# A fused attention and adapter kernel: the exchange of maxima and totals between two key classes moves to VectorE, and work is placed otherwise in two of its gaps

## The chip, the cores and the metric

The kernel runs on one core of a Trainium2 chip. The metric is the device time of one execution in microseconds (us). Five engines work side by side, each through its own queue in order: TensorE (PE; its weight loads are shown as PEld), VectorE (DVE), ScalarE (ACT), GpSimd (POOL) and the DMA queue (SP). They wait for each other by semaphores.

## The reference

Four sequences of 1024 tokens with 1024 features go through two blocks with a residual each, all in fp32:

```python
x = x + attn(layernorm(x), wq, wk, wv, wo)      # 32 heads of 32, rotary, causal softmax
x = x + ffn(layernorm(x), route_w, A, Bw)

# attn
q, k, v = split(x @ wq), split(x @ wk), split(x @ wv)
q, k = rotary(q), rotary(k)
scores = where(causal, q k^T / sqrt(32), min)
out = (softmax(scores) @ v) @ wo
# ffn: the best of 8 experts, weighted with its logit, rank 16
logits = x @ route_w^T
h = x @ A^T                                     # 8 experts x 16
out = (onehot(argmax(logits)) * max(logits) * h) @ Bw
```

## The kernel before

**Units.** The attention is cut into 32 units: 4 sequences of 8 groups of 4 heads. A unit has 16 query tiles `t` of 64 queries. Tile `t` has (t+1)*64 keys, and these are split in two classes, the even and the odd blocks of 32 keys. The 128 partitions of a score tile are two halves of 32 queries by two key classes: partition group `i = 2*half + odd` holds 32 queries against one class, and group `i ^ 1` holds the same queries against the other class. So the maximum and the total of a row of softmax each have to be joined from two partition groups. Tiles 0 to 7 make block 0 and tiles 8 to 15 block 1.

**A unit's slots.** `SLOTS` lists eleven slots of a unit. Nine are score rounds, `score_round` for one to four tiles: TensorE makes the scores (L381) in PSUM tile `s`, of which there is one; ScalarE copies them to SBUF (L392); GpSimd adds the causal mask on the diagonal (L395). Slot "second" multiplies block 1 of the unit before with its values (L565, in the same PSUM tile) and slot "first" block 0 of the unit itself. Numbered from 0, "second" is slot 2 and "first" slot 8; slot 3 has tiles 9, 2, 1 and 0.

**Softmax.** After a round, `find_tops` has VectorE reduce the negated maxima (L413) for the tiles that are complete. Four GpSimd copies of 32 partitions (L428) put each group's maxima into the partitions of the other class (`other`). In the next slot `join_tops` takes the minimum of both on VectorE (L433) and releases the tile's exponentials into `to_exp`. `exponentiate_some` issues them on ScalarE (L440) by a share, with their sums accumulated into `den`. `turn_probabilities` transposes them on VectorE (L465) at the beginning of a slot.

**Totals.** When all tiles of a block have been transposed, `join_sums` starts a generator, `sums_steps`. Its first half copies `den` across the classes on GpSimd (L505, four copies). Its second half runs in the next slot, from `go_on_with_sums`: VectorE adds (L507) and takes the reciprocal (L508) of 32 values a partition, and four GpSimd copies (L512) spread them to `by`. `spread_sums` turns `by` on TensorE (L539) behind the value product, ScalarE copies it back (L540), and `scale_values` multiplies on VectorE (L585) into `at`. As the value product lies in tile `s`, the next score round on TensorE waits for L585.

**What fills the gaps.** The list `todo` holds steps for TensorE: for the first sequence only the projections of the next unit, six chains of 8 steps (q, k for the first half of the tokens, q, k for the second, v for both; L295). A q or k chain ends with an eviction on ScalarE, two VectorE operations (L325, L327) and two GpSimd products of 128x512 (L326, L328) for the rotary embedding. `fill` runs a share of what is left of `todo` in each slot; for units 0 to 6 the share of slot r is `LENGTHS[r] / sum(LENGTHS[r:])`, for all others the slots count alike. In the later sequences `todo` also holds the output projection and the adapter of the sequence before. With two pieces of the value product ("second"), three steps are run between them.

**Norm of the next sequence.** The first four token tiles of sequence 1 are loaded at the start of unit 6. `Norm.scale(t)` finds the moments up to tile t+1 (VectorE, with one GpSimd power for each tile) and scales up to tile t. In unit 6, all four are scaled at once, as the `meanwhile` of `apply` in slot "first" (L981): behind the value product and ahead of `scale_values`. `turn` transposes them at the beginning of unit 7.

Of the kernel before, what the change touches and what calls it, by code (L numbers as in the profile page):

```python
# [9 lines left out]
F32 = mybir.dt.float32  # L10
AF = mybir.ActivationFunctionType
ALU = mybir.AluOpType
AX = mybir.AxisListType

P = 128
# [4 lines left out]
SQ = 32  # L20
# [6 lines left out]
    ((7, 0, 512), (6, 0, 448)),  # L27
    ((5, 0, 384), (4, 0, 320), (3, 0, 256)),
    "second",
    ((9, 0, 640), (2, 0, 192), (1, 0, 128), (0, 0, 64)),  # L30
    ((15, 0, 1024),),
    ((14, 0, 960),),
    ((13, 0, 896),),
# [11 lines left out]

LENGTHS = (1.6, 1.6, 0.5, 0.8, 0.8, 0.8, 0.8, 1.7, 1.4, 1.1, 1.3)


class Step:
# [20 lines left out]
def tile_preln_attn_then_top1_lora(  # L72
# [17 lines left out]
    nc = tc.nc  # L90
# [4 lines left out]
    HD = D // HEADS  # L95
# [303 lines left out]

    places, tops, dens = {}, {}, {}  # L400
    ended = []
    to_exp, to_turn, to_join, to_join_exp = deque(), [], [], []

    def find_tops(u):

        if not ended:
            return
        n = len(ended)
        top = small.tile([P, n, HG], F32, tag=f"top{n}", name=f"top_{u}_{ended[0]}", bufs=3)
        for k, t in enumerate(ended):  # L410
            step = HG if t < QT else 2
            for h in range(0, HG, step):
                nc.vector.tensor_reduce(  # L413
                    top[:, k, h : h + step],
                    places[u, t][:, h : h + step, :],
                    AX.X,
                    ALU.max,
                    negate=True,
                )
            tops[u, t] = top[:, k, :]  # L420
            if (u, t // QT) not in dens:
                dens[u, t // QT] = small.tile(
                    [P, QT, HG], F32, tag="den", name=f"den_{u}_{t // QT}", bufs=3
                )
        other = small.tile([P, n, HG], F32, tag=f"other{n}", name=f"other_{u}_{ended[0]}", bufs=2)
        for i in range(P // SQ):
            k = i ^ 1
            nc.gpsimd.tensor_copy(other[k * SQ : (k + 1) * SQ], top[i * SQ : (i + 1) * SQ])  # L428
        to_join.append((top, other))

    def join_tops():
        for top, other in to_join:
            nc.vector.tensor_tensor(top, top, other, ALU.min)  # L433
        to_join.clear()
        to_exp.extend(to_join_exp)
        to_join_exp.clear()

    def exponentiate(u, t, h):
        pr = places[u, t]
# [53 lines left out]
        ]  # L493
        return store, loads

    pending, wides = deque(), {}

    def sums_steps(u, blk):


        den = dens.pop((u, blk))
        other = small.tile([P, QT, HG], F32, tag="oden", name=f"oden_{u}_{blk}", bufs=2)
        for i in range(P // SQ):
            k = i ^ 1
            nc.gpsimd.tensor_copy(other[k * SQ : (k + 1) * SQ], den[i * SQ : (i + 1) * SQ])  # L505
        yield
        nc.vector.tensor_tensor(den, den, other, ALU.add)  # L507
        nc.vector.reciprocal(den, den)  # L508
        wides[u, blk] = by = big.tile([P, TB, P], F32, tag="by", name=f"by_{u}_{blk}")
        for i in range(P // SQ):  # L510
            rows = slice(i * SQ, (i + 1) * SQ)
            nc.gpsimd.tensor_copy(  # L512
                by[rows].rearrange("p t (h d) -> p t h d", d=HD),
                den[rows].rearrange("p (t c) h -> p c t h", c=2)[:, i % 2]
                .unsqueeze(3)
                .to_broadcast([SQ, TB, HG, HD]),
            )
        yield

    begun = set()  # L520

    def join_sums(u, blk):

        if (u, blk) in begun or any((u, t) in places for t in range(blk * QT, (blk + 1) * QT)):
            return
        begun.add((u, blk))
        pending.append(sums_steps(u, blk))
        next(pending[-1])

    def go_on_with_sums():  # L530
        while pending:
            next(pending.popleft())

    def spread_sums(u, blk):

        by = wides.pop((u, blk))
        pt = bank([P, TB, P], f"pr_{u}_{blk}")
        for i in range(TB):
            nc.tensor.transpose(pt[:, i, :], by[:, i, :], eye_sb)  # L539
        nc.scalar.copy(by, pt)  # L540
        return by.rearrange("p t k -> p (t k)")
# [259 lines left out]
    for u, (b, g) in enumerate(units):  # L801
        project, new_tail = [], []
        if b:
            fetch, (project,), new_tail = finish_steps(
                b - 1, g, "resident" if u == len(units) - 1 else "stream"
            )
            if g:
                between[-1].insert(max(0, len(between[-1]) - 8), fetch)
            else:
                late_fetch[u] = fetch  # L810

        if u + 1 < len(units) and g + 1 == NG:
            if b:
                homes = {0: "q", 1: "k", 3: "q", 4: "k"}
                norm = Norm(b + 1, {0: (3,), 1: (4,), 2: (6,), 5: (7,)}, homes)
                steps = change_steps(u + 1, norm, project, tail)
            else:
                norm = Norm(b + 1, {0: (5,), 1: (6,), 2: (7,)}, {4: "k"})  # L820
                between[-1].insert(0, Step(lambda norm=norm: norm.load(*range(TB)), 0.0))
                steps = [norm.turning(t) for t in range(TB)] + begin_steps(u + 1, norm, [])
            norms[b + 1] = norm
        else:
            steps = []
            if u + 1 < len(units):
                for n, tb in (("q", 0), ("k", 0), ("q", 1), ("k", 1), ("v", 0), ("v", 1)):
                    steps += chain(u + 1, n, tb)
            if not steps:
                steps = list(project)  # L830
            elif b and not g:
                steps = steps[:36] + weave(steps[36:], project)
            else:
                steps = weave(steps[:-6], project) + steps[-6:]
            if u + 1 == len(units):
                new_tail6 = tail
            n = len(steps)
            for k, s in reversed(list(enumerate(tail))):
                steps.insert(6 + k * n // 7, s)
        between.append(steps)  # L840
        tail = new_tail
# [85 lines left out]
    def apply(u, blk, meanwhile=lambda: None):  # L927
        while any((u, t) in places for t in range(blk * QT, (blk + 1) * QT)):
            exponentiate_some(1)
            turn_probabilities()  # L930
        join_sums(u, blk)
        go_on_with_sums()
        avs, pieces = value_pieces(u, blk)
        for k, piece in enumerate(pieces):
            piece()
            turn_probabilities()
            if k == 0:
                meanwhile()
            if k < len(pieces) - 1:
                exponentiate_some(VALUE_SHARE)  # L940
                do_some(APART_BY)
        by = spread_sums(u, blk)
        exponentiate_some(VALUE_SHARE)
        stores.append(scale_values(u, blk, avs, by))
# [9 lines left out]
    for u, (b, g) in enumerate(units):  # L954
# [6 lines left out]
            ends_at = second  # L961
        for r, pieces in enumerate(SLOTS):
            if pieces in ("first", "second"):
                join_tops()
            if pieces == "second":
                if u == final:
                    todo.extend(early)
# [9 lines left out]
                    meanwhile()  # L977
                stores.append(put)
            elif pieces == "first":
                if b == 0 and g + 2 == NG:  # L980
                    apply(u, 0, lambda: norms[1].scale(TB - 1))  # L981
                else:
                    apply(u, 0)
            else:
                join_tops()
                turn_probabilities()
                go_on_with_sums()
                if second < r < first_:
                    join_sums(u, 0)
                score_round(u, pieces)  # L990
                if r == second - 1 and u:
                    while any((u - 1, t) in places for t in range(QT, 2 * QT)):
                        exponentiate_some(1)
                        turn_probabilities()
                    join_sums(u - 1, 1)
                find_tops(u)
                exponentiate_some(SHARE / 3)
                to_join_exp.extend((u, t, h) for t in ended for h in range(HG))
                ended.clear()
                if r in (second + 1, first_ + 1):  # L1000
                    for put in stores:
                        put()
                    stores.clear()
                    if u == final and r == first_ + 1:
                        load_adapter()
                if r == second + 2:
                    scatter(loads, 2)
                    if u in late_fetch:
                        do(late_fetch[u])
                        for k in range(3 if b == 1 else 0):  # L1010
                            load_chunk(k)
# [11 lines left out]
                held_back,  # L1023
                0.0 if pieces in ("first", "second") else SHARE * 2 / 3,
            )
    join_tops()
    while to_exp:
        exponentiate_some(SHARE)
        turn_probabilities()
# [57 lines left out]
```

## Time and profile before

| | us |
|---|---|
| time, median of 3 runs (range) | 2867.87 (2865.06 to 2869.86) |
| the profiled execution: its time, its span | 2865.45, 2863.7 |
| busy: TensorE | 2718.6 (95%) |
| busy: VectorE | 1959.8 (68%) |
| busy: ScalarE | 1745.7 (61%) |
| busy: GpSimd | 1082.9 (38%) |
| VectorE waits for GpSimd's masks (L413 for L395) | 434.0, 193 times |
| VectorE waits for GpSimd's copies of maxima (L433 for L428) | 125.2, 138 times |
| first score matmul, last start of one | 65.4, 2757.9 |

The span is cut into units by the first score matmul of each. Units 0 to 6 begin at 65.4, 135.5, 210.5, 287.6, 362.8, 437.5 and 513.6 us, unit 7 at 599.6, unit 8 at 682.5. Units 8 to 14, 16 to 22 and 24 to 30 last 82 to 83 us each; the units with a change of sequence (15 and 23) 113.4 and 115.8 us.

How to read it: a busy share over the whole span hides that the sequences have different limits. The table of windows shows them apart. Where TensorE is busy nearly all of a window at full clock, only less work for it can shorten the window; where it is not, the list of its waits says who was late. The last column but two of a window line is the granted clock of TensorE, 1.00 at full speed.

### The profile page before, as it was taken

To read this page: it belongs to the slowest core of one execution; us is meant where nothing else is said; L and a number is where in the kernel's file an instruction comes from. 1 tells how busy PE (TensorE), PEld (TensorE's weight loads), DVE (VectorE), ACT (ScalarE), POOL (GpSimd) and SP (SyncE) were. 2 spreads that over 40 slices of the span, in tenths; PEclk is the share of its full clock that TensorE was granted. 3 is DMA by queue.
4 is the path that set the end of the run, shared out by engine and by line. 5 is a ranking of instruction groups with operands and counts; after the bars stand their busy time and mean duration, and the time that the engine had idled before them with its cause. 6 is when DMAs were issued, how large, how long until landed. Compare 5 with 4: busy or idle time off the path is not lost. (4 is left out here: it accounts for less than half of the span.)

```text
span 2863.7 us, 85129 instructions
## 1 busy us (share of the span) xinstructions
PE 2718.6 (95%) x35328; PEld 1343.4 (47%) x35328; DVE 1959.8 (68%) x3169; ACT 1745.7 (61%) x5006; POOL 1082.9 (38%) x2500
## 2 busy tenths in 40 slices
PE   8888898979999999998999999998999999999998
PEld 5344444444444444544445444444444445444445
DVE  3676666687776677777676776677667677776545
ACT  2676767756666666655666666664566666666421
POOL 3444444334334434333434334443344334334110
PEclk9999999989999999999999999999999999999999
DMA  3222222321555444363454455446154444454621
GB/s 113 49 54 46 53 53 49 83 68 39 159 142 141 124 134 134 112 194 83 105 148 116 121 140 141 126 132 186 45 151 135 128 127 118 119 142 136 175 65 52
DMA packets 448019, 317.92 MB, mean 111 GB/s; under 512 B 150288, under 2 KB 371728, under 8 KB 447632
## 3 DMA queue, kind: packets, MB, share of 16 engines
q1 hardware_dynamic: 447632, 312.47, 39.4%
q8 instruction: 278, 4.55, 0.7%
q14 instruction: 109, 0.89, 0.1%
HBM read 262.59 MB, written 49.81 MB: 109 GB/s over the span
## 5 line engine op out<-in xcount | busy, mean ns | idle before, releaser
L440 ACT ACTIVATE pr<-pr,top 128x256 f32<-128x256 f32 (+15 forms) x2048 | 1045.2, 518 | 92.1 <-DVE top L433 86.3
L413 DVE TENSOR_REDUCE top<-pr 128x2 f32<-128x960 f32 (+15 forms) x768 | 649.0, 896 | 434.4 <-POOL pr L395 434.0
L392 ACT COPY pr<-s 128x640 f32<-128x640 f32 (+14 forms) x544 | 525.5, 1018 | 556.0 <-PE s L381 555.6
L465 DVE STREAM_TRANSPOSE pr<-pr 128x1024 f32<-128x1024 f32 (+11 forms) x768 | 668.9, 905 | 33.1 <-ACT pr L440 32.8
L428 POOL COPY other<-top 32x4 f32<-32x4 f32 (+3 forms) x1152 | 249.3, 216 | 723.7 <-DVE top L413 688.1
L295 PE MATMUL pv<-xnT,wv 128*128 128x512 f32 x1024 | 491.0, 610 | 0.0
L295 PE MATMUL pq<-xnT,wq 128*128 128x512 f32 x1008 | 486.8, 609 | 3.3 <-ACT xnT L200 3.2
L295 PE MATMUL pk<-xnT,wk 128*128 128x512 f32 x1008 | 478.4, 605 | 1.1 <-ACT rawq L321 1.1
L395 POOL TENSOR_TENSOR pr<-pr,causal_sb 128x128 f32<-128x128 f32 x512 | 236.6, 472 | 562.4 <-ACT pr L392 551.0
L381 PE MATMUL s<-kT,qT 32*32 32x256 f32 (+4 forms) x17408 | 398.9, 392 | 49.8 <-DVE at L585 26.1
L440 ACT ACTIVATION_READ_ACCUMULATOR pr<-pr,top 128x1 f32 x2048 | 399.5, 195 | 0.0
L682 PE MATMUL po<-chunk,attn 128*128 128x512 f32 x736 | 377.1, 599 | 5.7 <-DMA chunk<-in_wo 5.7
L381 PEld LDWEIGHTS s<-kT,qT 32*32 32x32 f32 x17408 | 197.1, 103 | 315.5 <-issue 173.2
L295 PEld LDWEIGHTS pv<-xnT,wv 128*128 128x128 f32 x1024 | 190.8, 194 | 223.8 <-issue 218.5
L295 PEld LDWEIGHTS pk<-xnT,wk 128*128 128x128 f32 x1008 | 183.4, 192 | 237.3 <-issue 231.1
L295 PEld LDWEIGHTS pq<-xnT,wq 128*128 128x128 f32 x1008 | 184.4, 193 | 230.2 <-issue 224.4
L565 PE MATMUL av<-pr,vals 64*32 64x256 f32 (+3 forms) x12288 | 268.6, 318 | 0.0
L565 PEld LDWEIGHTS av<-pr,vals 64*32 64x32 f32 x12288 | 212.4, 105 | 105.4 <-issue 45.9
L682 PEld LDWEIGHTS po<-chunk,attn 128*128 128x128 f32 x736 | 135.1, 190 | 165.0 <-issue 139.9
L540 ACT COPY by<-pr 128x512 f32<-128x512 f32 x64 | 37.5, 585 | 268.3 <-PE pr L539 268.3
L512 POOL COPY by<-den 32x512 f32<-32x512 f32 x256 | 154.8, 605 | 110.7 <-DVE den L508 98.3
L433 DVE TENSOR_TENSOR top<-top,other 128x4 f32<-128x4 f32 (+3 forms) x288 | 86.8, 301 | 130.4 <-POOL other L428 125.2
(90 smaller groups left out, 1900.8 us busy)
## 6 DMA issues: line engine op xcount, KB each, us to landing
chunk<-in_wo SPq DMA_DIRECT2D x368, 256.0 KB, 3.6
vals<-vd SPq DMA_DIRECT2D x256, 128.0 KB, 4.2
x<-in_x SPq DMA_DIRECT2D x55, 512.0 KB, 4.4
wq<-in_wq SPq DMA_DIRECT2D x32, 512.0 KB, 4.1
wk<-in_wk SPq DMA_DIRECT2D x32, 512.0 KB, 4.7
wv<-in_wv SPq DMA_DIRECT2D x32, 512.0 KB, 4.3
vd<-vT SPq DMA_DIRECT2D x128, 128.0 KB, 5.2
out_y<-x SPq DMA_DIRECT2D x32, 512.0 KB, 2.9
```

The source lines that it names most:

```text
L295: nc.tensor.matmul(at["p"], lhsT=wt[:, c, :], rhs=xnTs[b][:, c, cols], start=(c == 0), stop=(c == NC - 1),)
L381: nc.tensor.matmul(sc[i * SQ : (i + 1) * SQ, h, at : at + w].rearrange("p (j k) -> p j k", k=SQ), lhsT=of_q[rows, 2 * t + half], rhs=of_k[ ...
L392: nc.scalar.copy(pr[:, :, k0 : k0 + w], sc[:, :, at : at + w])
L395: nc.gpsimd.tensor_tensor(diagonal, diagonal, causal_sb.unsqueeze(1).to_broadcast([P, HG, SQ]), ALU.add)
L413: nc.vector.tensor_reduce(top[:, k, h : h + step], places[u, t][:, h : h + step, :], AX.X, ALU.max, negate=True,)
L428: nc.gpsimd.tensor_copy(other[k * SQ : (k + 1) * SQ], top[i * SQ : (i + 1) * SQ])
L433: nc.vector.tensor_tensor(top, top, other, ALU.min)
L440: nc.scalar.activation(pr[:, h, :], pr[:, h, :], AF.Exp, bias=tops[u, t][:, h : h + 1], accum_out=dens[u, t // QT][:, t % QT, h : h + 1],)
L465: nc.vector.transpose(pr, pr)
L512: nc.gpsimd.tensor_copy(by[rows].rearrange("p t (h d) -> p t h d", d=HD), den[rows].rearrange("p (t c) h -> p c t h", c=2)[:, i % 2] .unsq ...
L565: nc.tensor.matmul(avs[half][h * HD : (h + 1) * HD, t0:, :], lhsT=v[rows, j, h * HD : (h + 1) * HD], rhs=rhs, start=(j == 0), stop=(j == n ...
L682: nc.tensor.matmul(st["po"], lhsT=lhsT, rhs=rhs, start=(c == start), stop=(c == stop))
```

## The change

Three parts. First, the exchange between the classes: VectorE reads the other class's values with the second input of a `tensor_tensor` of 32 partitions, four for each group of maxima (`both`) and four for each block's totals (`rec`). The GpSimd copies of both, the generator and its second half in a later slot are gone. The totals are only kept for the class that a partition group later needs, 16 values in place of 32, and one GpSimd copy of 128 partitions spreads them to `by`. The exponentials are released at the same points as before. Second, slot 3 has tile 9 last instead of first, and `LENGTHS` has other values. Third, the four tiles of sequence 1 are scaled by steps of `todo` in unit 6, each 8 projection steps after the one before, the first behind 16 of them, instead of all in slot "first".

```diff
@@ SLOTS
-    ((9, 0, 640), (2, 0, 192), (1, 0, 128), (0, 0, 64)),
+    ((2, 0, 192), (1, 0, 128), (0, 0, 64), (9, 0, 640)),
...
-LENGTHS = (1.6, 1.6, 0.5, 0.8, 0.8, 0.8, 0.8, 1.7, 1.4, 1.1, 1.3)
+LENGTHS = (4.4, 4.3, 2.6, 3.0, 4.3, 3.8, 3.8, 3.8, 2.8, 2.8, 3.3)
@@ find_tops
-        top = small.tile([P, n, HG], F32, tag=f"top{n}", name=f"top_{u}_{ended[0]}", bufs=3)
+        top = small.tile([P, n, HG], F32, tag=f"top{n}", name=f"top_{u}_{ended[0]}", bufs=2)
...
-        other = small.tile([P, n, HG], F32, tag=f"other{n}", name=f"other_{u}_{ended[0]}", bufs=2)
+
+        both = small.tile([P, n, HG], F32, tag=f"both{n}", name=f"both_{u}_{ended[0]}", bufs=3)
+        with_other(both, top, ALU.min)
+        for k, t in enumerate(ended):
+            tops[u, t] = both[:, k, :]
+
+    def with_other(dst, src, op):
+
         for i in range(P // SQ):
-            k = i ^ 1
-            nc.gpsimd.tensor_copy(other[k * SQ : (k + 1) * SQ], top[i * SQ : (i + 1) * SQ])
-        to_join.append((top, other))
-
-    def join_tops():
-        for top, other in to_join:
-            nc.vector.tensor_tensor(top, top, other, ALU.min)
-        to_join.clear()
-        to_exp.extend(to_join_exp)
-        to_join_exp.clear()
+            rows, other = slice(i * SQ, (i + 1) * SQ), slice((i ^ 1) * SQ, ((i ^ 1) + 1) * SQ)
+            nc.vector.tensor_tensor(dst[rows], src[rows], src[other], op)
+
+    def release_exps():
+        to_exp.extend(next_exp)
+        next_exp.clear()
@@ totals
-    def sums_steps(u, blk):
...
-    def go_on_with_sums():
-        while pending:
-            next(pending.popleft())
+    def join_sums(u, blk):
+
+
+        if (u, blk) in bys or any((u, t) in places for t in range(blk * QT, (blk + 1) * QT)):
+            return
+        den = dens.pop((u, blk)).rearrange("p (t c) h -> p c t h", c=2)
+        rec = small.tile([P, TB, HG], F32, tag="rec", name=f"rec_{u}_{blk}", bufs=2)
+        for i in range(P // SQ):
+            rows, other = slice(i * SQ, (i + 1) * SQ), slice((i ^ 1) * SQ, ((i ^ 1) + 1) * SQ)
+            nc.vector.tensor_tensor(rec[rows], den[rows, i % 2], den[other, i % 2], ALU.add)
+        nc.vector.reciprocal(rec, rec)
+        bys[u, blk] = by = big.tile([P, TB, P], F32, tag="by", name=f"by_{u}_{blk}")
+        nc.gpsimd.tensor_copy(
+            by.rearrange("p t (h d) -> p t h d", d=HD),
+            rec.unsqueeze(3).to_broadcast([P, TB, HG, HD]),
+        )
@@ the plan of unit 6
                 norm = Norm(b + 1, {0: (5,), 1: (6,), 2: (7,)}, {4: "k"})
+                for t in reversed(range(TB)):
+                    between[-1].insert(16 + 8 * t, norm.scaling(t))
                 between[-1].insert(0, Step(lambda norm=norm: norm.load(*range(TB)), 0.0))
@@ slots
-                join_tops()
+                release_exps()
...
-                if b == 0 and g + 2 == NG:
-                    apply(u, 0, lambda: norms[1].scale(TB - 1))
-                else:
-                    apply(u, 0)
+                apply(u, 0)
...
-                join_tops()
+                release_exps()
                 turn_probabilities()
-                go_on_with_sums()
                 if second < r < first_:
                     join_sums(u, 0)
```

More of the change, by code (lines that the diff above doesn't have):

```diff
@@ L401, in tile_preln_attn_then_top1_lora @@
     ended = []
-    to_exp, to_turn, to_join, to_join_exp = deque(), [], [], []
+    to_exp, to_turn, next_exp = deque(), [], []
     def find_tops(u):
@@ L419, in find_tops @@
                 )
-            tops[u, t] = top[:, k, :]
             if (u, t // QT) not in dens:
@@ L494, in spread_values @@
         return store, loads
-    pending, wides = deque(), {}
-    def sums_steps(u, blk):
-        den = dens.pop((u, blk))
-        other = small.tile([P, QT, HG], F32, tag="oden", name=f"oden_{u}_{blk}", bufs=2)
-        for i in range(P // SQ):
[L504 to L528, printed above, removed]
-    def go_on_with_sums():
-        while pending:
-            next(pending.popleft())
+    bys = {}
+    def join_sums(u, blk):
[3 more added lines that the diff above has]
+        rec = small.tile([P, TB, HG], F32, tag="rec", name=f"rec_{u}_{blk}", bufs=2)
+        for i in range(P // SQ):
+            rows, other = slice(i * SQ, (i + 1) * SQ), slice((i ^ 1) * SQ, ((i ^ 1) + 1) * SQ)
[6 more added lines that the diff above has]
+        )
     def spread_sums(u, blk):
-        by = wides.pop((u, blk))
+        by = bys.pop((u, blk))
         pt = bank([P, TB, P], f"pr_{u}_{blk}")
@@ L979, in tile_preln_attn_then_top1_lora @@
             elif pieces == "first":
-                if b == 0 and g + 2 == NG:
-                    apply(u, 0, lambda: norms[1].scale(TB - 1))
-                else:
-                    apply(u, 0)
+                apply(u, 0)
             else:
-                join_tops()
+                release_exps()
                 turn_probabilities()
-                go_on_with_sums()
                 if second < r < first_:
@@ L997, in tile_preln_attn_then_top1_lora @@
                 exponentiate_some(SHARE / 3)
-                to_join_exp.extend((u, t, h) for t in ended for h in range(HG))
+                next_exp.extend((u, t, h) for t in ended for h in range(HG))
                 ended.clear()
@@ L1025, in tile_preln_attn_then_top1_lora @@
             )
-    join_tops()
+    release_exps()
     while to_exp:
```

## The prediction

> **What bounds the kernel now.** I read the table of windows first, cut at the first score matmul of each unit. Columns: the window, its length, busy time (and instructions) of TensorE, its weight loads, VectorE, ScalarE, GpSimd, then the granted clock, DMA share and GB/s.
>
> ```profile
> 362.80:437.50 74.70, 67.86 (x1036) 31.98 (x1035) 51.43 (x79) 52.85 (x155) 32.13 (x76) 0.95 0.22 51
> ...
> 513.60:599.60 86.00, 69.18 (x1037) 32.48 (x1037) 60.70 (x99) 52.92 (x155) 35.76 (x80) 0.90 0.25 69
> ...
> 682.50:1256.90 574.40, 572.58 (x7623) 278.81 (x7622) 403.56 (x641) 375.25 (x1082) 230.82 (x539) 1.00 0.48 131
> ```
>
> Units 8 to 14 (last line) keep TensorE busy 99.7% at full clock: there the order of the other engines can gain nothing. The first sequence (units 0 to 6) is the loose part: 7 us idle in a unit, and a clock of 0.95, that is 10% of the time at half speed. Next, who TensorE waits for (time, times, longest):
>
> ```profile
> PE pr L539 <- POOL by L512: 27.5, 9, 8.9
> PE s L381 <- DVE at L585: 26.1, 25, 11.3
> ...
> PE s L381 <- ACT pr L392: 18.6, 14, 2.5
> ```
>
> The first two lie in the slot "first", the third in the score slots before it. The timeline of unit 4 from slot 7 shows the mechanism (TensorE, then VectorE, then GpSimd; start, length, instruction, idle time before it):
>
> ```profile
> 414.09 2.35 PE L565 MATMUL av<-pr,vals 64*32 64x256 f32 x128
> 419.38 0.66 PE L539 MATMUL pr<-eye_sb,by 128*128 128x128 f32 x4 [2.94 <-POOL by L512]
> 419.88 6.15 PE L295 MATMUL pv<-xnT,wv 128*128 128x512 f32 x10
> 427.38 1.49 PE L381 MATMUL s<-kT,qT 32*32 32x384 f32 x64 [1.35 <-DVE at L585]
> 428.80 3.70 PE L295 MATMUL pv<-xnT,wv 128*128 128x512 f32 x8
> ```
> ```profile
> 410.67 2.08 DVE L413 TENSOR_REDUCE top<-pr 128x2 f32<-128x896 f32 x2 [3.07 <-POOL pr L395]
> ...
> 413.76 0.16 DVE L433 TENSOR_TENSOR top<-top,other 128x4 f32<-128x4 f32 x1 [1.01 <-POOL other L428]
> ...
> 416.13 0.15 DVE L507 TENSOR_TENSOR den<-den,oden 128x32 f32<-128x32 f32 x1
> ...
> 419.89 1.95 DVE L413 TENSOR_REDUCE top<-pr 128x2 f32<-128x832 f32 x2 [3.23 <-POOL pr L395]
> ...
> 426.51 0.72 DVE L585 TENSOR_TENSOR at<-av,by 128x256 f32<-128x256 f32 x2
> ```
> ```profile
> 416.80 2.53 POOL L512 COPY by<-den 32x512 f32<-32x512 f32 x4 [3.07 <-DVE den L508]
> 419.41 0.45 POOL L395 TENSOR_TENSOR pr<-pr,causal_sb 128x128 f32<-128x128 f32 x1
> ```
>
> GpSimd runs in order. Its copies for the totals (L505, four of 0.2 us at 409.2, and L512, 2.53 us) stand in front of two masks (L395); VectorE waits 3.07 and 3.23 us for those, TensorE waits 2.94 us for `by` and 1.35 us for `at`.
>
> [...] L433's neighbours start 0.08 us after it, [...] L433 has minimum 151 and median 167 ns: [...]
>
> **Maxima (288 groups).** Removed: four GpSimd copies of 0.2 us, and VectorE's wait for them, 125.2 us in the waits of the whole run. Added: three more tensor_tensors a group; 4 x 0.165 = 0.66 us in place of 0.08 us of pitch, so +0.58 us, 167 us in all, against 125 us of wait [...]. VectorE's occupied time stays about level; it sits behind nothing new. Bounds for a group: 0.32 us if the four overlap, 1.9 us if one also meets a rope product. Taken: 0.66.
>
> **Totals (64 blocks).** Four copies of 0.20 and four of 0.605 us become one copy of 128x512, which I take at 0.6 us (bounds 0.6 and 2.4; each partition writes as many elements as before). Four small sums and a shorter reciprocal go on VectorE, +0.5 us. They run a round earlier, since the second half no longer waits for the next round. The new VectorE wait, for the last exponential's total, stands right behind the transposes, which wait for the same exponentials: nothing new is late. `by` is ready near 410 us instead of 419.3 in unit 4. The 27.5 us of TensorE waits for it go, and both masks come free. What is late next is `at`.
>
> **Gaps.** A step (two matmul records) costs 3.70/4 = 0.92 us. Working the planner's shares through 48 steps, a unit's slots 0, 1, 2 (in and behind "second"), 3 to 10 get 6, 6, 3+2, 3, 3, 3, 3, 6, 5, 4, 4 steps before and 5, 5, 3+3, 4, 5, 5, 4, 4, 3, 3, 4 after. Slots 3 to 7 lasted 26.7 us in unit 4 (387.4 to 414.1) with 18 steps; with 22, at full clock, TensorE needs 26.1 (22 x 0.92 = 20.3, score rounds 1.85 + 4 x 1.0). So their waits for ScalarE's evictions are filled and four steps leave other slots, which had no idle time: 3.7 us.
>
> Does `at` come in time? "first" now has 3 steps: the product ends at 415.8 (0.6 earlier), transposes 0.5, steps 2.8, so TensorE wants slot 9 at 419.1. VectorE from reduce 896 to `at` took 15.84 us; take away the waits for other and mask after that reduce (1.01 + 3.23), the den pair (0.5, a round earlier) and the k rope (1.45: its chain's step 32 moves from slot 7 to slot 6), add two joins (1.0): 10.7. That reduce can start between 408.7 (mask no longer behind oden) and 410.7; `at` ends 0.7 later, at 420.1 to 422.1. So 1 to 3 us of wait remain; I take 2.
>
> **A unit.** Units 1 to 5 (135.5 to 513.6) average 75.6 us, 8.5 idle, and lose 2.7 to the half clock (1 minus the clock, times the length): 64.4 without either. After: 64.4 + 2 (at) + 0.8 (one half-clock window every second unit) + 0.5 (score slots) = 67.7. Saved 7.9 x 5 = 39.5. Swapping the order in slot 3 lets tile 9's two reduces come last, behind its mask, while the small ones start during its eviction: ACT's 1.9 us wait at 397.12 shrinks; it is inside the 0.5.
>
> **Unit 0** (70.1 us): idle 10.9, of which one wait for `by` is 8.9, clock 0.95. Saved 9. **Unit 6**: the four scalings take 9.9 us of VectorE (577.37 to 587.25) ahead of `at`, and TensorE waits 11.3 for it. Spread over slots 3 to 8, VectorE's freed waits absorb some 4, so 6 remain on top of the usual 2: 86.0 becomes 76. Saved 10. **Elsewhere**: units 7, 15 and 23 wait for normalized tiles, whose VectorE queue is about level: 1 each. Units 8-14, 16-22 and 24-30 stay.
>
> Sum: 39.5 + 9 + 10 + 3 = 61.5. The profiled execution took 2865.45 us (span 2863.70), so 2804; the median shown, 2867.87, lies 2.4 higher, so 2806.
>
> **Rivals.** *B, VectorE becomes the first sequence's bound*: with 22 steps' time for slots 3 to 7 and only 3 in "first", `at` waits as long as before (4 to 5 us), since my count leaves VectorE nearly full there. For it: 52 of 68 us busy, and 10.5 us of mask waits in unit 4 that may not shrink. Against: the same work runs at 70% in units 8 to 14 without stalls. Then 67.7 becomes 71.5: 20 saved there, 6 in unit 0, 5 in unit 6: 2836. *C, the steps moved only move the stalls* (slots 0, 1 and 9 starve evictions instead): within 6 us of 2868; against it, ScalarE sat idle 0.2 to 2.3 us ahead of each eviction of those slots in unit 4. *D, slower*: the four held additions cost far more than 0.66 us[...]. Units 8-30 have 24.4 us of free VectorE ((574.40 - 403.56)/7), of which some 13.6 are waits for masks (434.0/32). Eleven groups a unit (9 maxima, 2 totals) fill the other 11 when each costs 1 us more; at 1.3 more (one rope product each time), 3.3 us x 21 units come on the path and half of A's gain goes: 2868 + 69 - 30 = 2907. For it: L433 of 128x12 averages 879 ns. Against: the new additions stand before the rope's products, not behind them.
>
> **Numbers.** A 0.66 (its own range 2785 to 2828), B 0.18, C 0.05, D 0.11. The range takes A and most of B, with the unknown start of the reduce: 2780 to 2846. A change below 0.2% can't be told from none. Faster 0.84, same 0.05, slower 0.11.
>
> **What would show it.** In the profile after: no wait of L539 for `by`; units 1 to 5 near 68 us, at a clock of 0.98 or more; one wait for `at` of 1 to 3 us a unit; the new tensor_tensors near 165 ns; units 8 to 14 unchanged at 82 us. Wrong if those lengthen, if the additions average over 400 ns, or if ScalarE's evictions stall slots 9 to 1.

## The result, and the profile after

| | before | after |
|---|---|---|
| time, median (range), same chip | 2866.48 (2865.06 to 2869.86) | 2842.57 (2839.23 to 2847.89) |
| ratio to before, 95% interval | | 0.9917 [0.9898, 0.9935] |
| profiled execution: its time, its span | 2865.45, 2863.7 | 2841.66, 2839.9 |
| units 1 to 5 | 378.1 | 365.2 |
| unit 0, unit 6 | 70.1, 85.9 | 65.0, 80.6 |
| units 7, 15, 23 | 83.0, 113.4, 115.7 | 85.9, 116.5, 115.9 |
| units 8-14, 16-22, 24-30 | 574.4, 579.9, 578.5 | 572.7, 577.4, 576.4 |
| busy: VectorE, GpSimd | 1959.8, 1082.9 | 2119.5, 711.7 |

The kernel became 0.8% faster, some 24 us. Forecast were 61.5 us. The measured time lies inside the predicted range, near its upper end and nearest to rival B (2836); it does so only because the range was drawn wide enough to take in most of B.

The table of windows after, cut as before at the first score matmul, for units 4, 6 and 7 and then units 8 to 14 (same columns as in the prediction):

```profile
351.40:423.30 71.90, 65.77 (x1033) 31.14 (x1032) 56.63 (x113) 52.94 (x154) 20.54 (x26) 0.95 0.22 53
495.10:575.70 80.60, 67.30 (x1033) 32.12 (x1032) 66.90 (x133) 52.92 (x154) 23.96 (x30) 0.92 0.27 74
575.70:661.60 85.90, 76.17 (x1098) 39.19 (x1098) 71.57 (x142) 57.82 (x165) 24.03 (x30) 0.94 0.25 69
661.60:1234.30 572.70, 572.45 (x7623) 276.73 (x7622) 437.94 (x873) 375.31 (x1083) 150.28 (x189) 1.00 0.48 131
```

Unit 4 (first line) fell from 74.7 to 71.9 us, where 67.7 were expected, and its clock is still 0.95, where at least 0.98 was expected. VectorE is busy 5.2 us longer in it than before, GpSimd 11.6 us less.

Who TensorE waits for after (in all, times, longest):

```profile
PE s L381 <- DVE at L568: 47.1, 8, 11.2
```

The wait for `by` (27.5 us) and the one for ScalarE's copies of the scores (18.6) are gone from the list. The wait for `at` has risen from 26.1 us in 25 places to 47.1 in 8: it left the steady units (8 to 14, 16 to 22, 24 to 30) and is now one wait in each of units 0 to 7, of 3.6 us in unit 0, 5.5 to 6.1 in units 1 to 5, 11.2 in unit 6 and 2.4 in unit 7. The timeline of unit 4, from the value product on TensorE (start, length, instruction, idle time before it):

```profile
401.01 2.35 PE L548 MATMUL av<-pr,vals 64*32 64x256 f32 x128
403.29 0.66 PE L522 MATMUL pr<-eye_sb,by 128*128 128x128 f32 x4
403.79 2.74 PE L295 MATMUL pv<-xnT,wv 128*128 128x512 f32 x6
412.65 2.37 PE L381 MATMUL s<-kT,qT 32*32 32x384 f32 x64 [6.13 <-DVE at L568]
```

VectorE in the same stretch, beginning two reductions before:

```profile
392.71 2.21 DVE L413 TENSOR_REDUCE top<-pr 128x2 f32<-128x960 f32 x2 [2.13 <-POOL pr L395]
...
397.49 0.76 DVE L509 TENSOR_TENSOR rec<-den 32x16 f32<-32x16 f32 x4
398.29 0.25 DVE L510 RECIPROCAL rec<-rec 128x16 f32<-128x16 f32 x1
399.73 2.08 DVE L413 TENSOR_REDUCE top<-pr 128x2 f32<-128x896 f32 x2 [1.19 <-POOL pr L395]
401.84 0.66 DVE L434 TENSOR_TENSOR both<-top 32x4 f32<-32x4 f32 x4
402.43 0.00 DVE L325 LOAD_MASK_SELECT swapk<-rawk  x1
402.54 0.76 DVE L325 STREAM_SHUFFLE swapk<-rawk 128x512 f32<-128x512 f32 x1
403.33 0.69 DVE L327 TENSOR_TENSOR swapk<-swapk,sin_sb 128x512 f32<-128x512 f32 x1
403.94 2.36 DVE L467 STREAM_TRANSPOSE pr<-pr 128x1024 f32<-128x1024 f32 x2
406.96 1.95 DVE L413 TENSOR_REDUCE top<-pr 128x2 f32<-128x832 f32 x2 [0.66 <-POOL pr L395]
408.94 0.66 DVE L434 TENSOR_TENSOR both<-top 32x4 f32<-32x4 f32 x4
409.63 2.24 DVE L467 STREAM_TRANSPOSE pr<-pr 128x960 f32<-128x960 f32 x2
411.79 0.72 DVE L568 TENSOR_TENSOR at<-av,by 128x256 f32<-128x256 f32 x2
```

And GpSimd:

```profile
398.67 0.61 POOL L512 COPY by<-rec 128x512 f32<-128x512 f32 x1 [6.00 <-DVE rec L510]
399.24 0.45 POOL L395 TENSOR_TENSOR pr<-pr,causal_sb 128x128 f32<-128x128 f32 x1
403.38 1.79 POOL L326 TENSOR_TENSOR rawk<-rawk,cos_sb 128x512 f32<-128x512 f32 x1 [3.68 <-DVE swapk L325]
405.25 1.27 POOL L328 TENSOR_TENSOR kT<-rawk,swapk 128x512 f32<-128x512 f32 x1
406.48 0.45 POOL L395 TENSOR_TENSOR pr<-pr,causal_sb 128x128 f32<-128x128 f32 x1
```

Read the last two fences side by side. The reduction at 399.73 waits for a mask; the mask stands behind the copy to `by`; the copy had waited 6.00 us for VectorE's `rec`. The reduction at 406.96 waits for a mask; the mask stands behind the two rope products; the first of them had waited 3.68 us for VectorE's shuffle. VectorE waits for GpSimd, which waits for VectorE: one chain through both engines. The minima (L434) stand in it: they come ahead of the shuffles and of `rec`, for which GpSimd waits. TensorE was done at 406.5 and waits until `at` comes.

The new instructions themselves cost what they were taken for (from the view of the line; shortest, median, longest in ns):

```profile
L434 DVE TENSOR_TENSOR both<-top x1152: 149/156/459, 70.1 to 2740.0; 32x4 f32<-32x4 f32 x128, 32x8 f32<-32x8 f32 x32, 32x12 f32<-32x12 f32 x32
```

### The profile page after: what moved, and what is told of

Same layout as the page of the kernel before. It is cut to its first block, busy times and chain, and to the rows that moved or that the text cites. A ratio compares the mean times of both kernels' runs of the same rounds, so it can differ in the third digit from the quotient of the medians.

```text
span 2839.9 us, 84110 instructions
## 1 busy us (share of the span) xinstructions
PE 2713.1 (96%) x35328; PEld 1334.1 (47%) x35328; DVE 2119.5 (75%) x4225; ACT 1746.1 (61%) x5006; POOL 711.7 (25%) x900
## 4 chain that ended last, share of the span: by engine, by line
PE 81%; DVE 10%; POOL 3%; DMA 2%; ACT 2%; issue 1%; SPq 0%; POOLq 0%; DVEq 0%; ACTq 0%
PE po L665 14%; PE pq L295 14%; PE pv L295 13%; PE pk L295 13%; PE s L381 12%; PE av L548 8%; DVE top L413 4%; DVE pr L467 2%; PE ph L686 2%; PE pf L725 2%; PE pr L522 1%; DVE both L434 1%; DMA chunk<-in_wo 1%; PE pt_f L198 1%; POOL pr L395 1%
## 5 line engine op out<-in xcount | busy, mean ns | idle before, releaser
L442 ACT ACTIVATE pr<-pr,both 128x256 f32<-128x256 f32 (+15 forms) x2048 | 1047.1, 520 | 40.4 <-DVE both L434 39.6
L395 POOL TENSOR_TENSOR pr<-pr,causal_sb 128x128 f32<-128x128 f32 x512 | 238.5, 472 | 1054.2 <-ACT pr L392 1045.4
L381 PE MATMUL s<-kT,qT 32*32 32x256 f32 (+4 forms) x17408 | 403.3, 395 | 48.7 <-DVE at L568 47.1
L442 ACT ACTIVATION_READ_ACCUMULATOR pr<-pr,both 128x1 f32 x2048 | 402.6, 197 | 0.0
L381 PEld LDWEIGHTS s<-kT,qT 32*32 32x32 f32 x17408 | 190.9, 104 | 306.9 <-issue 174.8
L434 DVE TENSOR_TENSOR both<-top 32x4 f32<-32x4 f32 (+3 forms) x1152 | 187.3, 163 | 23.7
L326 POOL TENSOR_TENSOR rawk<-rawk,cos_sb 128x512 f32<-128x512 f32 x64 | 114.1, 1784 | 289.0 <-DVE swapk L325 289.0
L326 POOL TENSOR_TENSOR rawq<-rawq,cos_sb 128x512 f32<-128x512 f32 x64 | 114.1, 1782 | 246.4 <-DVE swapq L325 246.4
```

The source lines that it names most:

```text
L326: nc.gpsimd.tensor_tensor(raw, raw, cos_sb[:, cols], ALU.mult)
L381: nc.tensor.matmul(sc[i * SQ : (i + 1) * SQ, h, at : at + w].rearrange("p (j k) -> p j k", k=SQ), lhsT=of_q[rows, 2 * t + half], rhs=of_k[ ...
L395: nc.gpsimd.tensor_tensor(diagonal, diagonal, causal_sb.unsqueeze(1).to_broadcast([P, HG, SQ]), ALU.add)
L434: nc.vector.tensor_tensor(dst[rows], src[rows], src[other], op)
L442: nc.scalar.activation(pr[:, h, :], pr[:, h, :], AF.Exp, bias=tops[u, t][:, h : h + 1], accum_out=dens[u, t // QT][:, t % QT, h : h + 1],)
```

## The experiments

Three theories were tested. By the first, `at` is late because of the order on the two engines, and small additions to VectorE are absorbed in its waits for masks. By the second, the four minima of each group are simply too much work for VectorE in the first sequence (rival B). The third was formed once the first four runs were read: the waits for masks are no slack, because VectorE and GpSimd feed each other in order, so that every link counts in full. A fifth is stated where it is first used. Each ratio below is to the kernel before on the same chip; the kernel after has 0.9917.

**`at` ahead of the transposes** (`e1_at_first`). In slot "first" the transposes of 2.24 us stand in front of `at`, although they release nothing that TensorE wants so soon.

```diff
@@ apply
-            turn_probabilities()
+            if len(pieces) > 1:
+                turn_probabilities()
...
         stores.append(scale_values(u, blk, avs, by))
+        turn_probabilities()
```

> The changed kernel, but in slot first the multiplication into at is issued on VectorE ahead of the transposes of finished exponentials (2.24 us in unit 4), which follow it. Theory 1 (order: what stands in VectorE's queue ahead of at sets the 6.1 us wait in slot first): the wait falls to about 3.9 us in units 1 to 5, units 69 to 70 us instead of 72, total 2822 to 2829. Theory 2 (amount: VectorE's work in a unit is the bound, wherever it stands): the wait comes back in slots 9 to 1, units 71 to 72, total 2838 to 2845.

Measured: 2828.44, ratio 0.9879 [0.9864, 0.9894]. The wait for `at` fell from 6.1 to between 4.1 and 4.3 us in units 1, 3, 4 and 5 (in unit 2 from 5.5 to 3.3); the units last between 69.1 and 72.2 us. The sum over the run (waits of TensorE):

```profile
PE s L381 <- DVE at L568: 30.0, 7, 9.1
```

What is taken off the chain ahead of `at` comes off the wait almost to its full length (2.0 of 2.2 us). It does not come off the unit to its full length: unit 4 fell by 0.7 us only, because TensorE was busy 67.06 us in it in place of 65.77. The granted clock of the profiled execution was 0.982 (0.983 after).

**The copy to `by` behind the mask** (`e1_mask_first`). Only GpSimd's order changes. The edit is shown in part: `spread_now` is also called ahead of the value products and ahead of the reductions of the slot before "second".

```diff
@@ join_sums
-        nc.gpsimd.tensor_copy(...)
+        to_spread.append((by, rec))
@@ slots
                 score_round(u, pieces)
+                spread_now()
```

> The changed kernel, but GpSimd's copy to by is issued behind the masks of the same slot instead of ahead of them. Theory 1: the reduce of tile 13 starts when VectorE is free, 1.2 us earlier, and the wait for at falls from 6.1 to about 4.9 us in units 1 to 5: total 2832 to 2838. Theory 2: under 0.3 us a unit, total 2840 to 2845.

Measured: 2830.43, ratio 0.9886 [0.9871, 0.9900]; the wait for `at` is 5.0 to 5.2 us (4.1 in unit 2), the units 71.3 to 71.7. A single instruction of 0.61 us, with its wait for `rec`, is worth about 1.1 us of the chain's end. Of the 7.1 us that units 1 to 5 gained together, 6.4 are in units 1 and 2; unit 4 gained 0.2.

**The minima twice** (`e1_double`). The four minima of each group are computed a second time into the same place; nothing else differs.

```diff
         with_other(both, top, ALU.min)
+        with_other(both, top, ALU.min)
```

> The changed kernel with the four small minima of each group issued twice, the second time with the same result: 0.62 us more VectorE work a group, nine groups a unit, five of them between the start of slot 3 and at. Theory 1: only the group of slot 7 stands directly ahead of at, the four before it are absorbed by VectorE's waits for masks (2.1, 1.2 and 0.7 us): the wait for at grows by 0.6 to 1 us, total 2846 to 2856 with the changes of sequence. Theory 2: it grows by 3.1 us, units 1 to 5 near 75 to 76 us, total 2865 to 2880. Units 8 to 14 stay at 82.3 us either way.

Measured: 2908.27, ratio 1.0157 [1.0133, 1.0181]. VectorE in unit 4:

```profile
409.46 2.21 DVE L413 TENSOR_REDUCE top<-pr 128x2 f32<-128x960 f32 x2 [2.13 <-POOL pr L395]
411.70 1.45 DVE L435 TENSOR_TENSOR both<-top 32x4 f32<-32x4 f32 x8
...
417.23 2.08 DVE L413 TENSOR_REDUCE top<-pr 128x2 f32<-128x896 f32 x2 [1.20 <-POOL pr L395]
```

Eight minima take 1.45 us, 0.79 more than four. The wait for `at` in unit 4 rose from 6.1 to 10.0 us: 3.9, five groups' 0.79. The bracketed waits for masks are as long as they were, 2.13 and 1.20 against 2.13 and 1.19: they absorbed nothing of work that stands ahead of the shuffle or of `rec`. Each of these waits is for an engine that itself waits for VectorE, and it moved along with the delay. That is against the first theory, which had the waits as slack; the second expected a longer wait, but 3.1 us and not 3.9. The units 8 to 14, which were to stay, grew from 572.7 to 581.6 us, and units 7, 15 and 23 by 16.7 together.

**The old gaps** (`e1_old_gaps`): the kernel after with the `LENGTHS` of before.

```diff
-LENGTHS = (4.4, 4.3, 2.6, 3.0, 4.3, 3.8, 3.8, 3.8, 2.8, 2.8, 3.3)
+LENGTHS = (1.6, 1.6, 0.5, 0.8, 0.8, 0.8, 0.8, 1.7, 1.4, 1.1, 1.3)
```

> The changed kernel with the shares of the gaps (LENGTHS) of before: slot first has 5 steps again, slots 4 to 6 three each. Theory 1: the wait for at shrinks by the two steps (1.8 us) to about 4, but 2 to 4 us of waits for evictions come back in slots 4 to 6: units 72 to 74 us, total 2842 to 2855. Theory 2: the same unit length as now, 72, total 2839 to 2846.

Measured: 2848.58, ratio 0.9950 [0.9934, 0.9965]. `at` waits 3.5 us, less than with the new gaps, but at the end of slot 5 TensorE waits 2.5 us for ScalarE's copy, and the granted clock of the profiled execution is 0.978 (0.983 after); a unit takes 75.0 us, more than either theory allowed. The new shares are worth about 0.33% of the run: they take fewer and longer stalls for more and shorter ones.

**The totals alone** (`e2_totals_only`): the kernel before with the new `join_sums` and without the old generator; maxima, gaps and scaling as before.

```diff
-    def sums_steps(u, blk):
...
-                go_on_with_sums()
+    def join_sums(u, blk):
...
+            nc.vector.tensor_tensor(rec[rows], den[rows, i % 2], den[other, i % 2], ALU.add)
```

> The kernel before with the new totals alone (four VectorE sums, one GpSimd copy, at once); maxima, gaps, order and scaling as before. If the totals' queue on GpSimd is what the change removes: no wait of TensorE for by, the wait in slot first falls from 4.3 to about 1.5 us (8.9 to about 2 in unit 0), units 1 to 5 near 73.5 us, total 15 to 22 us less than before. If the gain comes from the maxima: under 6 us less than before.

Measured: 2829.10, ratio 0.9884 [0.9869, 0.9898], some 34 us saved, where 15 to 22 were expected. Units 1 to 5 gave 14.2 of them, unit 0 gave 9.0 and the steady units 7.1. Waits of TensorE:

```profile
PE s L381 <- DVE at L566: 26.0, 8, 12.6
```

There is no wait for `by`; the one for `at` is 2.4 us in unit 4. One part of the change alone gives more than the whole change.

**The maxima through GpSimd** (`e2_maxima_pool`): the kernel after with the four GpSimd copies and the one minimum of before.

```diff
-        with_other(both, top, ALU.min)
+            nc.gpsimd.tensor_copy(other[k * SQ : (k + 1) * SQ], top[i * SQ : (i + 1) * SQ])
...
+            nc.vector.tensor_tensor(top, top, other, ALU.min)
```

> The changed kernel with the maxima exchanged by GpSimd copies and joined in the next slot, as before; totals, gaps, order and scaling as changed. Theory 3 (from slot 3 to at, VectorE and GpSimd form one serial chain, in which a wait for a mask is no slack because the rope products in front of the mask wait for VectorE themselves): the 2.9 us of small minima go, but waits of 1 us for the copies come in their place unless VectorE has other work there; wait for at 4 to 7 us, total within 10 us of the changed kernel. Theory 2 (only VectorE's busy time counts): wait for at about 3.2 us, total 18 to 25 us less than the changed kernel, and the changes of sequence return to 113 to 115 us.

Measured: 2828.23, ratio 0.9877 [0.9861, 0.9893]. Waits of TensorE:

```profile
PE s L381 <- DVE at L566: 45.3, 8, 10.0
```

The wait for `at` in unit 4 is 5.9 us against 6.1, although VectorE is busy 52.4 us there in place of 56.6: the amount of VectorE's work doesn't set it. Waits of about 1.0 us for the copies are back in three of the five groups ahead of `at`. The gain is elsewhere: 83.7, 114.2 and 113.5 us for units 7, 15 and 23 against 85.9, 116.5 and 115.9, 2.2 us in unit 6, and 6.1 us in units 1 to 5 together. Of these 6.1, unit 2 has 4.1 and units 3 to 5 together 0.7; they are not shown to be the minima's. On the same chip the totals alone gave 0.9884, so that beside the old maxima gaps and scaling add nothing that can be told from none.

**The maxima alone** (`e3_maxima_only`): the kernel before with that one part of the change.

```diff
-            nc.gpsimd.tensor_copy(other[k * SQ : (k + 1) * SQ], top[i * SQ : (i + 1) * SQ])
-            nc.vector.tensor_tensor(top, top, other, ALU.min)
+        with_other(both, top, ALU.min)
```

> The kernel before with the maxima alone exchanged on VectorE; totals, gaps, order and scaling as before. The prediction's step (level: 167 us more VectorE work against 125 us of waits [...]): within 6 us of before. Theory 5 (the four held minima cost time wherever VectorE's queue is the last to arrive, that is in slot first and in the units with a change of sequence; the waits that they replace were mostly no loss): 8 to 18 us more than before, units 7, 15 and 23 together 5 to 8 us longer.

Measured: 2892.35, ratio 1.0090 [1.0074, 1.0106], 25 us slower, more than the 8 to 18 expected. The wait of TensorE for `at`, then the window of units 8 to 14:

```profile
PE s L381 <- DVE at L587: 41.6, 25, 11.8
```
```profile
688.50:1267.60 579.10, 572.27 (x7623) 278.80 (x7622) 436.82 (x831) 374.12 (x1083) 186.19 (x287) 1.00 0.47 130
```

TensorE's busy time is as before (572.27 against 572.58), yet the window is 4.7 us longer: in 18 of the 21 steady units `at` comes 1.0 us late instead of 0.3. The steady units lose 13.3 us together, units 0, 6, 7, 15 and 23 another 12.1, units 1 to 5 only 0.2. Most of the added work was absorbed: in units 8 to 14 VectorE is busy 33.3 us longer, for 4.7 us more time.

**The rope products behind the mask** (`e2_rope_late`): in units 1 to 7 the two GpSimd products wait until the next round's masks have been issued.

```diff
@@ rope
-            nc.gpsimd.tensor_tensor(raw, raw, cos_sb[:, cols], ALU.mult)
             nc.vector.tensor_tensor(other, other, sin_sb[:, cols], ALU.mult)
-            nc.gpsimd.tensor_tensor(dst[:, cols], raw, other, ALU.add)
+            rotations.append(rotate)
@@ slots
                 score_round(u, pieces)
+                rotate_now()
```

> The changed kernel with GpSimd's two rope products of a projection of units 1 to 7 issued behind the masks of the next score round instead of ahead of them. Theory 3: VectorE's waits for masks behind rope products (1.3, 2.1 and 0.7 us in unit 4) go, and the wait for at falls from 6.1 to 2 to 4 us, total 15 to 25 us less than the changed kernel. Theory 2: VectorE's amount of work is the same, the wait stays above 5.5 us, total within 5 us of the changed kernel.

Measured: 2854.85, ratio 0.9969 [0.9958, 0.9980]: slower than after. The wait for `at` went to 4.8 us as the chain would have it, but 2.6 us of waiting came up at the end of slot 5. VectorE shows from where:

```profile
384.21 0.01 DVE L332 LOAD_MASK_SELECT swapk<-rawk  x1 [8.40 <-POOL qT L337]
```

The shuffle of k waits 8.40 us for q's last product. The rope tiles have three buffers, and q's, put off across slot "second", which has no score round, still held one.

**All three together** (`e2_all_three`): the three edits on the kernel after, GpSimd's order being mask, `by`, rope.

> The changed kernel with at ahead of the transposes, by behind the masks and the rope products behind the masks. Theory 3: the three savings add up (2.0 and 1.1 us as measured, 2 to 4 for the rope), so the wait for at is 0 to 1 us and units 1 to 5 last 65 to 67 us: total 2790 to 2808. Theory 2: the time comes back in other slots, units 69 to 71 us, total 2820 to 2830.

Measured: 2814.16, ratio 0.9825 [0.9808, 0.9842]. Unit 4 takes 67.5 us; what is left of waits is 1.3 us at the end of slot 5, 0.4 behind it and 1.2 us for `at`. The total missed the expected 2790 to 2808. The buffer's wait is still there, 5.78 us.

**The buffers freed** (`e3_three_dve` with the new maxima, `e3_three_pool` with those of before): the put-off products are also issued at the beginning of slots "first" and "second".

```diff
+            if pieces in ("first", "second"):
+                rotate_now()
             if pieces == "second":
```

> The kernel of e2_all_three, with rope products that still wait issued at the beginning of the slots first and second too, so that the three buffers of the rotary embedding come free before the k chain needs one. If the buffers made VectorE wait 5.8 us in slot 3: no wait in slots 5 and 6, wait for at under 0.5 us, units 1 to 5 at 65 us, total 2800 to 2808. If not: as e2_all_three, 67.5 us and 2812 to 2818.

> The kernel of e3_three_dve with the maxima exchanged by GpSimd copies and joined in the next slot. Theory 5: units 7, 15 and 23 are shorter by 5 to 8 us together, and VectorE has 2.9 us less in slots 3 to 8: total 2788 to 2800. Rival: the copies stand in front of masks again, units 1 to 5 are 2 us longer: total 2805 to 2815.

Measured: 2793.43, ratio 0.9749 [0.9731, 0.9767], and 2782.74, ratio 0.9710 [0.9694, 0.9726], both below what was expected. In both, units 4 and 5 take 64.3 us without a wait of TensorE, and the granted clock of the profiled execution is 0.990 and 0.989 (0.983 after). Unit 4 of `e3_three_pool` in the table of windows, and what is left of the wait for `at` in the whole run:

```profile
320.60:384.90 64.30, 64.30 (x1039) 30.63 (x1040) 51.36 (x85) 52.79 (x155) 26.63 (x62) 1.00 0.25 60
```
```profile
PE s L394 <- DVE at L586: 4.9, 1, 4.9
```

TensorE is busy all of the 64.30 us, at a granted clock of 1.00. With the minima on VectorE the unit is as short, although VectorE is then busy 57.5 us in it, more than in the kernel after. What the minima cost here is mostly in units 7, 15 and 23 (7.1 us together) and unit 6 (2.2); units 1 to 5 differ by 0.4 in all. `e3_three_pool` beats both kernels, before by 2.9%, and takes nothing from the change's minima.

**The scaling at once** (`e3_scale_once`): the kernel after with the four scalings back in slot "first" of unit 6.

```diff
-                for t in reversed(range(TB)):
-                    between[-1].insert(16 + 8 * t, norm.scaling(t))
...
-                apply(u, 0)
+                if b == 0 and g + 2 == NG:
+                    apply(u, 0, lambda: norms[1].scale(TB - 1))
+                else:
+                    apply(u, 0)
```

> The changed kernel with the four tiles of the second sequence scaled at once in slot first of unit 6, as before. The prediction's step (VectorE's freed waits absorb 4 us of the 9.9): unit 6 longer by 4 us, total 2843 to 2849. Theory 3 (VectorE and GpSimd are one serial chain up to at, so it doesn't matter where the 9.9 us stand ahead of at): unit 6 within 2 us, total within 4 us of the changed kernel.

Measured: 2840.99, ratio 0.9915 [0.9897, 0.9933], the same as after. TensorE ahead of slot 9 of unit 6, in this kernel and then in the kernel after:

```profile
563.57 2.47 PE L381 MATMUL s<-kT,qT 32*32 32x384 f32 x64 [16.00 <-DVE at L568]
```
```profile
563.66 2.57 PE L381 MATMUL s<-kT,qT 32*32 32x384 f32 x64 [11.24 <-DVE at L568]
```

Spread, the scaling takes 4.8 us off the wait for `at`. Of these, 2.1 have only moved: TensorE now waits 2.06 us for ScalarE ahead of the value product. The other 2.7 agree with two waits of VectorE for masks behind the rope products: 2.12 and 0.65 us long with the scaling at once, they are gone with the scaling spread, because a part of it stands behind the shuffles. So it does matter where the scaling stands: a wait does absorb work that is placed behind what the other engine waits for. Little of it reaches the unit (81.8 us against 80.6, one profiled execution each), as TensorE is busy 67.3 us in place of 65.8, and over the run the difference can't be told from nothing.

## Why the prediction was right and wrong

**Totals: the mechanism right.** `by` was ready at 399.3 us in a unit that began at 351.4, 47.9 in; before it came at 419.3, 56.5 in. TensorE's 27.5 us of waits for it are gone, the copy takes 0.611 us (0.6 taken), and the part alone brings 34 us.

**Maxima: the price right, the balance wrong.** A group costs 0.66 us as taken; that each of its four minima adds its whole length was the author's estimate, which no trace of the kernel before showed. Wrong was what was set against it: "VectorE's occupied time stays about level; it sits behind nothing new." With this part alone, VectorE's busy time rose by 149.4 us (2109.2 against 1959.8) while 125.2 us of waits for the copies went: 24 us up instead of level, and the profiled span grew by 24.2. In units 1 to 5 of the kernel before it did come out level (0.2 us); the time was lost in the steady units, in units 0 and 6 and at the changes of sequence. Within the changed kernel the part costs some 0.4% (0.9917 against 0.9877). The estimate of level, and the prices with one rope product in them, counted on the long additions of L433 in the kernel before: a mean of 301 ns at a median of 167, 38 us over 288 additions. In that trace 50 of them began while a rope product (L326) ran and took 0.30 to 1.26 us, 21 while a mask (L395) ran and took 0.41 to 0.42, the other 217 took 0.15 to 0.18.

**Gaps: the steps right, `at` wrong.** This is the largest miss: units 1 to 5 gained 12.9 us together instead of 39.5. Slots 3 to 7 of unit 4 lasted 25.8 us without a wait, where 26.1 were worked out, and TensorE wanted slot 9 at 31.3 us behind slot 3's start, where 31.7 were. But `at` was 6.1 us late instead of 2. The 4.1 us come from three terms. The reduction of 896 elements began 24.5 us behind slot 3's start, where 21.3 to 23.3 were allowed (2.2 beyond the middle): "both masks come free" did not hold, one stood behind `by` and the others behind the ropes. The stretch from there to `at` took 12.06 us instead of 10.7: the k rope pair (1.45 us) stayed in it, for its chain did move to slot 6, but the reduction of 896 elements is that slot's own and is issued ahead of the slot's steps; a wait of 0.66 us for a mask behind the ropes came on top, and the transposes were 1.0 us shorter. And TensorE was 0.4 us earlier. So the failed step is the answer to "Does `at` come in time?": a start of the reduction with the masks free, and 10.7 us from there, which treated waits for GpSimd as removable one by one. In their place the runs show one chain through both engines, with `at` 6.1 us late.

**Half clock.** Taken were 0.8 us a unit, one window in every second unit, by the author's estimate. The clock records of the trace have two windows of 3.4 us at a granted clock of 0.50 in each of units 1, 3, 4 and 5 (in unit 4 from 409.3 to 416.1) and three in unit 2: eleven in units 1 to 5, where the kernel before had eight. What sets them off is not shown. Of unit 4's 71.9 us, 64.3 are work at full clock (shown by the last experiments; 64.4 were worked out) and 6.1 the wait: 1.5 us are the clock's. Against the 67.7 of the sum that is 4.1 more for `at` and 0.7 more for the clock, while the 0.5 for waits in score slots did not come.

**Unit 0, unit 6 and the rest.** Unit 0 gained 5.1 of 9 and unit 6 5.3 of 10. In unit 0 3.6 us of waiting for `at` are left, in unit 6 11.2, against 11.3 before. That VectorE's waits would absorb some 4 us of the scaling was right in kind: they absorbed 2.7. Wrong was "the usual 2" below it, which is about 6 here as in units 1 to 5, and the new wait ahead of the value product was not foreseen. Units 7, 15 and 23, put at 1 us gained each, lost 6.2 together, and the experiment with the maxima on GpSimd takes 6.9 off them (318.3 to 311.4): VectorE's queue ahead of the normalized tiles was not level. The 21 steady units, put at nothing, gained 6.3: most of it is their waiting for `at`, 0.3 us in each of 18 of them, which went away.

**Rivals.** B's time was nearest, but its reason falls: VectorE is idle 15.3 of 71.9 us in unit 4, taking the minima from it leaves `at` where it was, and with as much work on VectorE but another order (`e3_three_dve`) the wait is gone. C's stalls did not come either: TensorE has no wait for copies of scores left. A cost of the sort that D priced did come, but thinly: of the 1152 minima 27 took longer than 250 ns, each beside a mask (L395), and none longer than 459. What did become longer are GpSimd's rope products (see the last section).

**The reason in its place.** From slot 3 to `at` in units 1 to 5, VectorE and GpSimd form one serial chain. Shown: links taken out of it shorten it (2.0 us for the transposes, 1.1 for `by`), a link added ahead of the shuffles lengthens it in full (3.9 us), and with `at`, `by` and the rope products moved and the buffers freed there is no wait (64.3 us), minima or not. Not shown: why the minima cost time in the steady units and how the loss in units 7, 15 and 23 is made up. Not tried: the new order in slot 3 by itself.

## What to carry to other kernels

When one engine waits for another, look at what the releaser itself had waited for: two engines that run in order and feed each other make one chain, and their waits are not slack for work that stands ahead of what the other engine waits for; work placed behind that can go into them. On the engine that serves such a chain, put the short products that nobody wants yet behind the one that somebody waits for, and count the buffers that postponing holds. Measure the parts of a change by themselves: here one of them was worth more than the whole, and another took a third of the gain back. And a wait that is shortened need not shorten the run by as much: here 2.0 us less of waiting made unit 4 0.7 us shorter.

## What was unexpected of the hardware

Four minima that read other partitions than they write took 0.66 us, starting 0.165 us apart and lasting 0.15 to 0.16 each, so that none began before the one ahead had ended. In the kernel before, the instruction behind L433 at 413.76 (0.16 us long) had started at 413.84. In `e1_double`, eight into the same tile started 0.18 us apart; why so is open.

The first rope product on GpSimd (L326 in both kernels), before and then after, from the view of the line (shortest, median, longest in ns):

```profile
L326 POOL TENSOR_TENSOR rawk<-rawk,cos_sb x64: 1261/1277/1784, 35.1 to 2627.8; 128x512 f32<-128x512 f32 x64
```
```profile
L326 POOL TENSOR_TENSOR rawk<-rawk,cos_sb x64: 1772/1783/1793, 34.5 to 2601.9; 128x512 f32<-128x512 f32 x64
```

Every one that began while VectorE's product with two inputs (L327) was running took 1.59 to 1.80 us, every other one 1.26 to 1.30. The excess, 0.3 to 0.5 us, was less than what was left of VectorE's product when the rope product began (0.47 to 0.65 of its 0.69 us). Before, 46 of the 128 began so; after, all 128 do, 44 us more of GpSimd in all: with its copies gone, GpSimd stands ready when the shuffle ends (it waited for the shuffle 41 times before and 128 times after), just as VectorE starts its own product (403.33 and 403.38 in the fences above). The prediction did not count this, and it lies in the chain ahead of the masks; what it costs by itself was not tried.
